# Product quantized convolution on one core: half products of four outputs in a row, and layer 2's preparation moved into layer 1's tail

## The chip, the cores and the metric

The kernel runs on one core of a Trainium2 chip. The metric is the device time of one execution in microseconds. Before the change it is 3702.62 us, the median of three runs (3702.26 to 3704.74).

## The reference

The input x has shape (32, 1024, 14, 14), in fp32. Two residual blocks follow each other. The first, and the only one that the change touches, is a bottleneck of three product quantized ("amm") convolutions, each followed by a batch norm over images and pixels:

```python
def _amm(patches, centroids, lut, inv_temp):
    v = patches.reshape(B, ncb, sub, H * W).transpose(0, 3, 1, 2)
    scores = 2.0 * jnp.einsum('blcs,cks->blck', v, centroids) - jnp.sum(centroids * centroids, -1)[None, None]
    attn = jax.nn.softmax(scores * inv_temp, axis=-1)
    out = jnp.einsum('blck,cko->blo', attn, lut)
    return out.transpose(0, 2, 1).reshape(B, -1, H, W)

out = _amm(x, c1_centroids, c1_lut, c1_invt)             # 1024 -> 256, 256 codebooks of 4 values
out = jax.nn.relu(_bn(out, bn1_g, bn1_b))
out = _amm(_extract3x3(out, 1), c2_centroids, c2_lut, c2_invt)   # 3x3, 256 codebooks of 9 values
out = jax.nn.relu(_bn(out, bn2_g, bn2_b))
out = _amm(out, c3_centroids, c3_lut, c3_invt)           # 256 -> 1024, 64 codebooks of 4 values
out = _bn(out, bn3_g, bn3_b)
return jax.nn.relu(out + identity)

x = x + _L0_conv_ref(_gn(x), ...)    # the block above
x = x + _L1_conv_ref(_gn(x), ...)    # linear attention with rotary positions, and a depthwise 3x3
```

Each codebook has K = 16 centroids: the scores go through a softmax over 16, and its weights multiply rows of a table (`lut`).

## The kernel before, in words

**Stages.** Layers 1, 2 and 3 of the first block run one after the other, each with a batch norm in between, and then the attention block. The order of the instructions on every engine in the three layers is the order in which the program emits them (`manual_schedule`); each engine and each DMA queue works through its own list in order and waits where an operand is missing. The attention block is ordered by a planner (`Plan`), which the change does not touch.

**Layers 1 and 2.** Their work is cut into 128 units: 16 pairs of images (392 pixels) times 8 groups of codebooks. `units` (line 701) interleaves the steps. For a unit, TensorE makes four score tiles of 128 (codebook, centroid) rows in PSUM; ScalarE takes the exponential with a bias (`exponentials`, line 563); DVE transposes so that the 16 centroids lie next to each other (`token_major`), sums over them, takes the reciprocal and transposes it back; GpSimd multiplies (`softmax`, line 585). The softmax weights of a codebook sum to one, so one of the 16 table rows is subtracted from the others (`less`, a matmul with the fixed matrix `less_last` and a copy on ScalarE), and the freed rows hold weights of other codebooks: `spare_rows` (line 691) moves these with small DMAs on the SP queue, and `others` and `keep` in `packed_lut` do the same for the table. Then `lut` adds up table times weights in two PSUM banks. Scores run 4 units (layer 1) or 3 units (layer 2) ahead of the table products, so that the table product of unit u waits only for work that began several units before. `side(i)` and `side2(i)` are called once per unit and place all other work: loads, norms, next tables.

**From layer 1 to layer 2.** After the last unit of layer 1 its norm is finished (`bn_final`). `store_pair` (line 907) applies norm and relu on ScalarE into a padded picture and stores it to DRAM three times, shifted, by SP; `load_patches` (line 933) reads from there what the 3x3 windows need, twelve DMAs for each half of the channels of a pair. Two pieces cannot be taken from these patches alone: the score of layer 2 is a sum of four matmuls of 64 rows on the patches (eight taps, matrix `w8`) and four of 32 rows on the padded picture (the ninth tap, matrix `wm`). The biases (`score_biases`), `w8` (`score_matrices`) and `wm` are made on DVE, between the first patches and the first score. Tables 0 to 3 of layer 2 are reduced (`less`) there too, tables 4 to 7 in `side2`. ScalarE issues a part of the first patches' DMAs, SP all others.

**Layer 3.** The 6272 pixels are cut into 14 chunks of 448. The two groups of codebooks (b = 0, 1) of chunk k + 1 are scored (`score3`, line 1087; four matmuls of 32 rows side by side) while chunk k is multiplied. The freed rows leave seven full tiles of 128 weight rows and one of 64. `spread3` fills the freed rows by small DMAs; `double3` copies the 64 rows of the first tile into its other 64, in two DMAs. A chunk has eight outputs of 128 channels. An output is the sum of seven whole products (`whole`) and a half product of 64 rows. The outputs are taken two at a time (m0 = 0, 2, 4, 6): one half product uses the upper 64 rows and the other the lower 64, so that TensorE does both at once:

```python
for m0 in range(0, CT, 2):
    ...
        whole(m0)
    for m in (m0, m0 + 1):
        r = slice(64 * (m - m0), 64 * (m - m0) + 64)
        product(m, 0, r, ...)
        whole(m0 + 1)
```

After a pair, ScalarE copies the outputs out of PSUM and DVE gathers statistics. The first scores (b = 0) of the next chunk stand before the chunk's first output, the second (b = 1) after output 0; their softmax follows outputs 1 and 3. PSUM has four banks for scores, three for products and one (`ps_tr`) for small things.

Of the kernel before, what the change touches and what calls it, by code (L numbers as in the profile page):

```python
# [10 lines left out]
F32 = mybir.dt.float32  # L11
AF = mybir.ActivationFunctionType
ALU = mybir.AluOpType
# [4 lines left out]
P = 128  # L18
C = 1024
CT = C // P  # L20
# [130 lines left out]
def conv_preact_kernel(ctx: ExitStack, tc: tile.TileContext, a: dict, out: bass.AP):  # L151
# [177 lines left out]
    SHIFT = 32.0  # L329

    def centre(pool, i, name, v, k):

        rows, groups = v.shape[:2]
        mean = pool.tile([rows, groups], F32, tag=f"cmean{i}{name}", name=f"cmean{i}{name}")
        t = pool.tile([rows, 1], F32, tag=f"cinvt{i}{name}", name=f"cinvt{i}{name}")
        nc.vector.tensor_scalar(t, invs[i][:rows], k, None, ALU.mult)
        nc.vector.tensor_reduce(mean, v, AX.X, ALU.add)
        nc.vector.tensor_scalar(mean, mean, t, 1.0 / KC, ALU.mult, ALU.mult)
        nc.vector.scalar_tensor_tensor(v, v, t, bc(mean, 2, KC), ALU.mult, ALU.subtract)

    def score_matrices(pool, i, name, raw, mask):


        rows, groups = raw.shape[:2]
        w = pool.tile([rows, groups, P], F32, tag=f"cw{i}{name}", name=f"cw{i}{name}")
        centre(pool, i, name, raw, 2.0)
        for g in range(0, groups, 4):
            m = min(4, groups - g)
            nc.vector.tensor_tensor(
                w[:, g : g + m].rearrange("p g (c k) -> p g c k", k=KC),  # L350
                raw[:, g : g + m].unsqueeze(2).to_broadcast([rows, m, 8, KC]),
                mask.unsqueeze(1).unsqueeze(3).to_broadcast([rows, m, 8, KC]),
                ALU.mult,
            )
        return w

    def score_biases(ps_tr, pool, tmp, i, raw, rows, groups, mask, per, order=None):

# [12 lines left out]
        cols = sq  # L371
        bias = pool.tile([P, n], F32, tag=f"cbias{i}", name=f"cbias{i}")
        nc.vector.tensor_copy(spread.rearrange("p (c k) -> p c k", k=KC), bc(mask, 2, KC))
# [12 lines left out]
        def biases():  # L386
# [5 lines left out]
            nc.vector.tensor_tensor(pv, pv, bc(kmask, 1, n), ALU.mult)  # L392
            b = pool.tile([P, n], F32, tag=f"cb{i}", name=f"cb{i}")
            nc.vector.tensor_reduce(b, pv, AX.X, ALU.add)
# [96 lines left out]
    def layers(exact, early=None):  # L491
# [143 lines left out]
        tsp = two.enter_context(tc.tile_pool(name="p12t", bufs=1))  # L635

        def unit_tiles(n):

# [61 lines left out]

        def units(ahead, ts, pool, luts, score, bias, dst, stats, side, last, halve=False):

# [27 lines left out]
            for i in range(-ahead, n):  # L730
# [8 lines left out]
                if 0 <= u < n:  # L739
# [4 lines left out]
                        *tts.pop(u),  # L744
                        spare=spares[u // 4 % 2] if u % 4 == 0 else None,
                    )
                    spare_rows(ts, u)
# [12 lines left out]
        with ExitStack() as s:  # L760
            once = s.enter_context(tc.tile_pool(name="p1c", bufs=1))
            xp = s.enter_context(tc.tile_pool(name="p1x", bufs=3))
            sm = s.enter_context(tc.tile_pool(name="p1s", bufs=2))
# [11 lines left out]
            def load(p):  # L775
                def piece():
                    xts[p] = load_x(xp, p)
                    v = slice(2 * p, 2 * p + 2)
# [59 lines left out]
            for b in range(2):  # L838
                luts[b][1]()
            xts[1] = load_x(xp, 1)  # L840
            for b in range(2, 8):
# [31 lines left out]
            def score1(u):  # L873
                p, b = divmod(u, 8)
                scs = []
                for j in range(4):
# [3 lines left out]
                    scs.append(sc)  # L880
                return scs

            units(
# [15 lines left out]
        with ExitStack() as s:  # L899
# [51 lines left out]
            luts2[7][1]()  # L951
            load_patches(0, 0, 1, engines=(nc.sync, nc.scalar))
            store_pair(0, 1)
            luts2[2][2]()
            load_patches(0, 1, 3)
            luts2[3][2]()
            for b in range(4):
                luts2[b][4]()
            bias2, biases = score_biases(
                ps_tr,  # L960
                once,
                st,
                2,
                raw[2],
                72,
                32,
                mask2,
                1,
                lambda t, src=False: t.rearrange("p (h j b) -> p h b j", h=2, j=4)
                if src  # L970
                else t.rearrange("p (h b j) -> p h b j", h=2, b=4),
            )
            w8 = score_matrices(once, 2, "8", raw8, mask64)
            biases()
            warm(5, pads[0][:, :N2])

            centre(once, 2, "1", raw1, 2.0)
            wm = once.tile([P, 2, 4, P], F32, tag="wm", name="wm")
            for h in range(2):
                nc.vector.tensor_tensor(  # L980
                    wm[:, h].rearrange("p b (c k) -> p b c k", k=KC),
                    raw1[:, h].unsqueeze(1).unsqueeze(2).to_broadcast([P, 4, 8, KC]),
                    mask32.rearrange("p (b c) -> p b c", c=8)
                    .unsqueeze(3)
                    .to_broadcast([P, 4, 8, KC]),
                    ALU.mult,
                )

# [30 lines left out]
            def side2(i):  # L1019

                for b in range(4, 8):
                    if i == max(b - 7, -ahead):
                        luts2[b][2]()
                    if i == max(b - 4, 0):
                        luts2[b][4]()
                if i == max(-2, -ahead):
                    luts2[4][3]()
                if i == -ahead:
# [12 lines left out]
            def next_lut3(b):  # L1041
# [15 lines left out]
                side2,  # L1057
                lambda h: bn_final(once, stats2, 2, [h], sc2, bi2),
            )
            next_lut3(7)  # L1060
# [5 lines left out]
        with ExitStack() as s:  # L1066
# [78 lines left out]
            relu3(1, 1)  # L1145
            nxt = [score3(1, 0)]
            rows = sum(map(split3, t3), [])
# [6 lines left out]
            spread3(rows, range(4, 8))  # L1154
            double3(rows[0])
            for k in range(NCH):
                more = k + 1 < NCH
                if more and k:
                    nxt = [score3(k + 1, 0)]
                elif not more and not exact:  # L1160
                    add_up(2, 2 * NCH)
                    again = overflow(once)
# [5 lines left out]
                def product(m, g, r=slice(0, P), start=False, stop=False):  # L1168
# [6 lines left out]
                    )  # L1175

                def whole(m):
                    for g in range(1, CT):
                        product(m, g, start=m % 2 == 0 and g == 1, stop=m % 2 == 1 and g == 7)

                for m0 in range(0, CT, 2):
                    for m in range(m0, m0 + 2 + (k + m0 == 0)):
                        if m not in pos:
                            pos[m] = ps_po.tile([P, 512], F32, tag="po", name="po3")[:, :NC]

                    if k + m0 == 0:
                        for g in range(1, CT):
                            for m in range(3):
                                product(m, g, start=g == 1)
                    elif k > 0 or m0 != 2:  # L1190
                        whole(m0)
                    for m in (m0, m0 + 1):
                        r = slice(64 * (m - m0), 64 * (m - m0) + 64)
                        product(
                            m, 0, r, start=m > m0 and k + m0 > 0, stop=m == m0 or k + m0 == 0
                        )
                    if k + m0 > 0:
                        whole(m0 + 1)
                    for m in (m0, m0 + 1):
                        nc.scalar.copy(o[:, m, :], pos[m])  # L1200
                        nc.vector.bn_stats(stats3[:, m, k, :], o[:, m, :])  # L1201
                        if not more:
                            bn_sum(mv3[:, m, :], stats3, m)
                        if more and m == 0:
                            nxt.append(score3(k + 1, 1))
                        if m in (4, 5):
                            relu3(k + 2, m - 4)
                        if more and m in (1, 3):
                            t = nxt[m // 2]
                            softmax(st, 2 * k + 2 + m // 2, t, *token_major(st, t))  # L1210
                            if m == 1:
                                then = split3(t)
                                spread3(then, (1, 2, 3))
                            else:
                                then += split3(t)
                                spread3(then, range(4, 8))
                                double3(then[0])
                nc.sync.dma_start(o3d[:, :, k * NC : (k + 1) * NC], o)
                if more:
                    rows = then  # L1220
            bn_final(once, None, 3, range(CT), sc3, bi3, mv3)
# [804 lines left out]
```

## Time and profile before

| what | us |
|---|---|
| median of three runs | 3702.62 |
| the profiled execution, own time | 3700.99 |
| its span | 3699.2 |
| TensorE busy | 3626.1 |
| DVE busy | 2979.5 |
| GpSimd busy | 2307.5 |
| ScalarE busy | 1717.9 |
| layer 1's last table product ends, TensorE's next work begins | 836.7 |
| first score of layer 2 | 856.3 |
| first scores of layer 3 | 1845.1 |
| first product of layer 3 | 1860.3 |
| last chunk's products begin | 2501.4 |

In the lines of the profile, PE is TensorE, PEld its loading of weights, DVE VectorE, ACT ScalarE, POOL GpSimd, and SPq and ACTq the DMA queues that SyncE and ScalarE issue. In a timeline line the first number is the start in us from the span's beginning and the second its length; then come engine, line of the kernel, instruction, what it writes and reads with shapes, and the number of instructions that were merged into the line. In brackets stands how long the engine idled before and what released it. In a group line the numbers after the bar are busy us in all and the mean ns of one instruction, then the idle time before them. An fp32 matmul is recorded as two instructions, one for each of its two passes, each with a load of weights.

### The profile page before, as it was taken

The page shows a single profiled execution, that of the slowest core. Times are in us where ns is not written, and L with a number is a line of the kernel's source. Part 1 is how long each engine was busy: PE and PEld are TensorE (multiplying, and loading weights), DVE is VectorE, ACT ScalarE, POOL GpSimd, SP SyncE. Part 2 cuts the span into 40 slices and gives each one's busy share as a digit, 9 for nine tenths or more (in the row PEclk, how much of TensorE's full clock was granted, in tenths as well). Part 3 has the DMA queues.
Part 4 walks back from the last instruction along what each step waited for, and adds up shares of the span by engine and source line. Part 5 has one row for each costly group of instructions (what it writes and reads, how often), then busy time and mean ns, then how long its engine had stood idle before and what let it go on. Part 6 is the DMA issues. An engine that isn't in the chain of part 4 may idle for free. (4 is left out here: it accounts for less than half of the span.)

```text
span 3699.2 us, 49702 instructions
## 1 busy us (share of the span) xinstructions
PE 3626.1 (98%) x16229; PEld 1999.0 (54%) x16229; DVE 2979.5 (81%) x4291; ACT 1717.9 (46%) x3895; POOL 2307.5 (62%) x1398
## 2 busy tenths in 40 slices
PE   8999999999999999999999999998999999999999
PEld 4555555554554445445444444444666666666666
DVE  8999999987888888888753334333799999999996
ACT  5555555543333333333322222213776676676675
POOL 6999999993454445445421111111988888888887
PEclk9999999999999999999999999999999999999999
DMA  3111111115444434444221111103123233233321
GB/s 110 43 46 44 43 37 32 43 33 134 89 92 87 94 75 94 85 95 84 72 51 53 45 45 45 38 33 130 44 79 93 82 87 91 86 84 85 90 75 44
DMA packets 238331, 260.14 MB, mean 70 GB/s; under 512 B 33380, under 2 KB 235692, under 8 KB 238064
## 3 DMA queue, kind: packets, MB, share of 16 engines
q1 hardware_dynamic: 237280, 256.51, 26.2%
q8 instruction: 131, 2.15, 0.3%
q14 instruction: 136, 1.11, 0.1%
q10 hardware_dynamic: 784, 0.37, 0.0%
HBM read 164.04 MB, written 77.09 MB: 65 GB/s over the span
## 5 line engine op out<-in xcount | busy, mean ns | idle before, releaser
L612 POOL TENSOR_TENSOR t<-t,r 128x1664 f32<-128x1664 f32 (+3 forms) x288 | 1008.5, 3502 | 952.0 <-DVE r L605 771.7
L717 PE MATMUL po<-t,lut 128*128 128x392 f32 x3840 | 1332.1, 499 | 2.7 <-DMA t<-spare 2.5
L717 PEld LDWEIGHTS po<-t,lut 128*128 128x128 f32 x3840 | 710.5, 190 | 593.3 <-issue 122.0
L566 ACT ACTIVATE t<-sc,cbias 128x392 f32<-128x392 f32 (+1 forms) x1136 | 580.0, 594 | 946.2 <-issue 476.1
L1536 PE MATMUL mm<-y,lut 128*128 128x392 f32 x2048 | 710.4, 493 | 0.1
L1169 PE MATMUL po<-t,lut 128*128 128x448 f32 (+1 forms) x1792 | 662.1, 551 | 1.6 <-issue 1.6
L578 DVE STREAM_TRANSPOSE tt<-t 128x1664 f32<-128x1664 f32 (+1 forms) x284 | 541.8, 1908 | 105.4 <-ACT t L566 99.7
L605 DVE STREAM_TRANSPOSE r<-rc 128x1664 f32<-128x1664 f32 (+1 forms) x284 | 546.5, 1924 | 20.8 <-DVE rc L599 0.5
L1758 DVE SCALAR_TENSOR_TENSOR pa<-y,lepe_w,pa 128x406 f32<-128x406 f32 x900 | 537.4, 637 | 3.8 <-PE pa L1740 0.3
L1536 PEld LDWEIGHTS mm<-y,lut 128*128 128x128 f32 x2048 | 370.4, 188 | 243.1 <-issue 6.1
L1169 PEld LDWEIGHTS po<-t,lut 128*128 128x128 f32 (+1 forms) x1792 | 308.7, 189 | 352.0 <-issue 351.3
L597 DVE TENSOR_REDUCE sm<-tt 128x104 f32<-128x832 f32 (+2 forms) x284 | 423.2, 1490 | 7.6 <-POOL tt L581 2.0
L1201 DVE BATCH_NORM_STATS2 stats<-o 128x6 f32<-128x448 f32 x112 | 68.9, 617 | 432.0 <-ACT o L1200 432.0
L581 POOL TENSOR_TENSOR tt<-tt 128x832 f32<-128x832 f32 x128 | 248.4, 1941 | 9.3 <-DVE tt L578 9.3
L599 DVE RECIPROCAL rc<-sm 128x104 f32<-128x104 f32 (+1 forms) x284 | 229.4, 808 | 9.8
L1200 ACT COPY o<-po 128x448 f32<-128x448 f32 x112 | 59.2, 530 | 326.4 <-PE po L1169 278.5
L999 PE MATMUL sc<-patch,cw 64*128 64x392 f32 x1024 | 204.0, 514 | 1.4 <-ACT lut L675 1.4
L614 ACT ACTIVATE sm<-sm 128x104 f32<-128x104 f32 (+1 forms) x284 | 84.9, 299 | 215.3 <-DVE rc L599 213.6
L999 PEld LDWEIGHTS sc<-patch,cw 64*128 64x128 f32 x1024 | 87.5, 184 | 109.5 <-issue 62.0
L1721 POOL TENSOR_TENSOR qr<-qr,zb 128x784 f32<-128x784 f32 x64 | 117.8, 1852 | 42.7 <-DMA zb<-zd 35.1
L1389 ACT ACTIVATE w<-x,tb,gn_a 128x196 f32<-128x196 f32 x248 | 128.3, 517 | 33.4 <-DVE x L1403 19.9
L1545 ACT ACTIVATE e<-mm,kbd 128x392 f32<-128x392 f32 x128 | 74.6, 583 | 145.2 <-PE mm L1536 143.7
(191 smaller groups left out, 4103.7 us busy)
## 6 DMA issues: line engine op xcount, KB each, us to landing
patch<-h1d SPq DMA_DIRECT2D x248, 162.8 KB
x<-in_x_dram SPq DMA_DIRECT2D x32, 784.0 KB
o3d<-o SPq DMA_DIRECT2D x14, 1792.0 KB
x<-in_x_dram SPq DMA_DIRECT2D x64, 392.0 KB
out_dram<-x SPq DMA_DIRECT2D x64, 392.0 KB
o<-o3d SPq DMA_DIRECT2D x62, 392.0 KB
h1d<-pad SPq DMA_DIRECT2D x96, 225.0 KB
t<-spare SPq DMA_DIRECT2D x960, 12.2 KB
```

The lines of the kernel that those rows point to most:

```text
L566: nc.scalar.activation(t[:, j, : sc.shape[1]], sc, AF.Identity if exact else AF.Exp, bias=bias[:, j : j + 1],)
L578: nc.vector.transpose(tt, tf)
L581: nc.gpsimd.tensor_tensor(tv[:, :, :8], tv[:, :, :8], tv[:, :, 8:], ALU.add)
L597: nc.vector.tensor_reduce(sm, tv, AX.X, ALU.add)
L599: nc.vector.reciprocal(rc, sm)
L605: nc.vector.transpose(r, bc(rc, 2, KC))
L612: nc.gpsimd.tensor_tensor(tf[:, v], tf[:, v], r[:, v], ALU.mult)
L717: nc.tensor.matmul(po[h], luts[b][:, j, h * P : (h + 1) * P], ts[u % len(ts)][:, j, :N2], start=(b == 0 and j == j0), stop=(b == 7 and j = ...
L999: nc.tensor.matmul(sc, w8[r, 8 * h + 4 * (j // 2) + g], grid(pbuf[n % NPB][r, j // 2, g]), start=True, stop=False,)
L1169: nc.tensor.matmul(pos[m], luts[g][r, m * P : (m + 1) * P], rows[g][r], start=start, stop=stop,)
L1536: nc.tensor.matmul(pv(), w[kt][:, m0 : m0 + P], ywin(p, first + kt), start=(kt == 0), stop=(kt == 3),)
L1758: nc.vector.scalar_tensor_tensor(acc, neighbours(p, c, offset(k)), lw[:, c, k : k + 1], acc, ALU.mult, ALU.add,)
```

## The change

It has four parts.

1. **Layer 3: halves of four outputs together.** The outputs are taken four at a time (m0 = 0, 4). The order on TensorE is: the whole products of m0, the scores of the next chunk (b = 0 with m0 = 0, b = 1 with m0 = 4), the half products of m0 to m0 + 3, then the whole products of the other three. The softmax of the scores follows the copy and statistics of output m0. The fourth output in work uses the bank of `ps_tr`. In chunk 0 the first four outputs have their whole products first and their halves last.
2. **Layer 2's matrices in layer 1's tail.** `matrices2` makes `w8`, `wm` and the biases at step 125 of layer 1's 128 steps (the bias matmul at step 127), in a tile that a third of layer 1's x tiles used before; `Cut` hands out pieces of a tile. Layer 1's x ring of three becomes a ring of two and a pool of one that lasts through layer 2.
3. **First patches by two queues.** The remaining three quarters of the first patches are issued by SP and ScalarE too, before the second `store_pair`. Tables 2 to 7 are reduced one step or more later in `side2`; `warm` has eight matmuls instead of five.
4. **First weights in pieces.** The GpSimd multiplication of layer 2's units 0 and 1 is split into three pieces each.

```diff
-            xp = s.enter_context(tc.tile_pool(name="p1x", bufs=3))
+            xp = s.enter_context(tc.tile_pool(name="p1x", bufs=2))
...
-                    xts[p] = load_x(xp, p)
+                    xts[p] = load_x(kept if p % 3 == 1 else xp, p)
...
+            def matrices2():
+                room = kept.tile([P, CT, N2], F32, tag="x", name="room2")
...
+                cut = Cut(st.tile([P, 4 * NCP], F32, tag="tt", name="cut2", bufs=n))
+                bias2, biases = score_biases(
...
+                parts[2] = score_matrices(cut, 2, "8", raw8, mask64, w8), wm, bias2
+                centre(cut, 2, "1", raw1, 2.0)
+                for h in range(2):
+                    nc.vector.tensor_tensor(
+                        wm[:, h].rearrange("p b (c k) -> p b c k", k=KC),
...
+                at(8 * NP - 1, biases)
+
+            at(8 * NP - 3, matrices2)
...
-            load_patches(0, 0, 1, engines=(nc.sync, nc.scalar))
+            both = nc.sync, nc.scalar
+            load_patches(0, 0, 1, engines=both)
+            load_patches(0, 1, 3, engines=both)
             store_pair(0, 1)
-            luts2[2][2]()
-            load_patches(0, 1, 3)
-            luts2[3][2]()
-            for b in range(4):
-                luts2[b][4]()
-            bias2, biases = score_biases(
...
-            w8 = score_matrices(once, 2, "8", raw8, mask64)
-            biases()
-            warm(5, pads[0][:, :N2])
...
+            luts2[0][4]()
+            luts2[1][4]()
+            warm(8, pads[0][:, :N2])
+            w8, wm, bias2 = parts[2]
...
-                for b in range(4, 8):
-                    if i == max(b - 7, -ahead):
+                for b in range(2, 8):
+                    if i == max(b - 6 if b > 2 else -3, -ahead):
                         luts2[b][2]()
-                    if i == max(b - 4, 0):
+                    if i == max(b - 3 if b > 3 else b - 4, -ahead):
                         luts2[b][4]()
-                if i == max(-2, -ahead):
-                    luts2[4][3]()
+                    if b == 4 and i == -1:
+                        luts2[4][3]()
...
+                steps={0: (1, 1, 1), 1: (1, 1, 2)},
...
-            nxt = [score3(1, 0)]
+            nxt = score3(1, 0)
...
                 def whole(m):
                     for g in range(1, CT):
-                        product(m, g, start=m % 2 == 0 and g == 1, stop=m % 2 == 1 and g == 7)
+                        product(m, g, start=m % 4 == 0 and g == 1, stop=m % 4 > 0 and g == 7)
+
+                def halves(m0):
+                    for m in (m0, m0 + 1):
                         if m not in pos:
+                            pool, tag = (ps_tr, "tr") if m % 4 == 3 else (ps_po, "po")
+                            pos[m] = pool.tile([P, 512], F32, tag=tag, name="po3")[:, :NC]
+                        r = slice(64 * (m - m0), 64 * (m - m0) + 64)
+                        first = k + m0 // 4 == 0
+                        product(m, 0, r, start=m % 4 > 0 and not first, stop=m % 4 == 0 or first)
...
+                for m0 in (0, 4):
...
+                        whole(m0)
+                    t = None
+                    if more and (k or m0):
+                        t = score3(k + 1, m0 // 4)
+                    elif more:
+                        t = nxt
+                    halves(m0)
+                    halves(m0 + 2)
+                    out(m0)
+                    if t is not None:
+                        then(m0 // 4, t)
+                    for m in range(m0 + 1, m0 + 4):
+                        if k + m0 > 0:
+                            whole(m)
+                        out(m)
```

## The prediction

> **What bounds the kernel now.** I read the page's shares first, then TensorE's groups with shapes kept apart, then the timeline in the two places that the change touches. The page:
>
> ```profile
> span 3699.2 us, 49702 instructions
> ...
> PE 3626.1 (98%) x16229; PEld 1999.0 (54%) x16229; DVE 2979.5 (81%) x4291; ACT 1717.9 (46%) x3895; POOL 2307.5 (62%) x1398
> ```
>
> TensorE is busy for 98% of the span, and only 73 us are idle anywhere. So a saving needs less TensorE time in a stage, or less idle time at a joint. TensorE's groups in layer 3, by form:
>
> ```profile
> L1169 PE MATMUL po<-t,lut 128*128 128x448 f32 x1568 | 612.5, 545 | 1.6 <-issue 1.6
> L1169 PE MATMUL po<-t,lut 64*128 64x448 f32 x224 | 57.3, 588 | 0.0
> L1093 PE MATMUL sc<-out,cw 32*128 32x448 f32 x224 | 29.0, 586 | 1.3 <-ACT out L1083 1.3
> ```
>
> Every product counts twice here (14 chunks x 8 outputs x 7 rows = 784, shown as 1568): fp32 runs in two passes. Layer 3 practically never waits; only its TensorE work can shrink. What a block of short matmuls costs is seen in the weight loads, whose starts give the beat (timeline, weight loads of layer 3):
>
> ```profile
> 2062.21 0.19 PEld L1169 LDWEIGHTS po<-t,lut 128*128 128x128 f32 x1 [0.19 <-issue]
> 2063.05 0.30 PEld L1169 LDWEIGHTS po<-t,lut 64*128 64x128 f32 x4 [0.65 <-issue]
> 2064.01 0.30 PEld L1169 LDWEIGHTS po<-t,lut 128*128 128x128 f32 x2 [0.65 <-issue]
> 2064.49 0.19 PEld L1169 LDWEIGHTS po<-t,lut 128*128 128x128 f32 x1 [0.19 <-issue]
> ```
>
> Full passes follow each other every 0.375 us. Around a pair of half products the starts are 0.84, 0.96 and 0.48 us apart: 2.28 us instead of 3 x 0.375 = 1.125. So a block of one half pair adds 1.16 us, of which two passes (0.75) are work and 0.41 is the change into half rows and back. A block of scores (32 rows, four side by side) has the same gaps, 0.85 and 0.96, at 2069.47. A chunk holds four half blocks and two score blocks: 112 x 0.375 + 6 x 1.16 = 49.0 us, and chunk periods by the timeline are 49.02 us (2057.59 to 2106.61). The model holds.
>
> Does a second half pair right behind the first pay the change again? Layer 2 shows it:
>
> ```profile
> 1502.51 0.96 PEld L999 LDWEIGHTS sc<-patch,cw 64*128 64x128 f32 x8 [0.56 <-issue]
> 1504.03 0.31 PEld L1008 LDWEIGHTS sc<-pad,wm 32*128 32x128 f32 x8 [0.56 <-issue]
> 1504.90 1.28 PEld L717 LDWEIGHTS po<-t,lut 128*128 128x128 f32 x5 [0.56 <-issue]
> ```
>
> Eight 64-row loads lie within 0.96 us, of which the last group takes 0.30: the second pair starts 0.66 us after the first, two passes at layer 2's 0.328. So nothing is paid between pairs. From the second pair to the 32-row block it is 1504.03 - 1503.17 = 0.86 us, 0.20 more than two passes: changing between 64 and 32 rows costs 0.20.
>
> The other place is the start of layer 2 (timeline, several engines):
>
> ```profile
> 842.54 4.48 ACTq L940 DMA_DIRECT2D patch<-h1d  x6
> 847.07 0.71 ACT L909 ACTIVATE pad<-out,bi,sc 128x392 f32<-128x392 f32 x1 [6.17 <-DMA patch<-h1d]
> 856.34 0.96 PEld L999 LDWEIGHTS sc<-patch,cw 64*128 64x128 f32 x8 [0.56 <-DVE wm L980]
> 858.81 2.02 ACT L566 ACTIVATE t<-sc,cbias 128x392 f32<-128x392 f32 x4 [7.81 <-PE sc L1008]
> 880.08 4.74 PE L717 MATMUL po<-t,lut 128*128 128x392 f32 x12
> 887.14 2.93 PEld L717 LDWEIGHTS po<-t,lut 128*128 128x128 f32 x10 [0.56 <-issue]
> ```
>
> The first score waits for DVE's wm, the last matrix of layer 2. Its patches are there long before: by windows of half a microsecond the DMA burst that carries them ends at 848.5. From 880 on (first table product) TensorE runs without gaps, unit after unit of 7.85 us; 887.14 is unit 1's first product, my mark for the joint.
>
> **What the Trainium skill says.** "TensorEngine Tiling (Array Packing)", Key Properties: changing the tiling mode, not just the tile, drains TensorE. The trace agrees: 0.41 us out and back, nothing between two 64-row pairs. "TensorE: Matmul & The Clock Gate", Part 3, says that tiles of different row groups run side by side; four 64-row loads within 0.30 us agree. "DMA: Bandwidth & Descriptors", Issuing engines are not separate DMA queues: a second issuing engine saves only issue time. Here twelve loads take 6.16 us on SP alone (849.67) and six on each of SP and ACT 4.48 us, while the DMA engines are busy 0.8 to 0.9 at 180 to 190 GB/s (852 to 858): I count little for the second queue.
>
> **The change part by part.**
>
> *Layer 3.* Per half chunk, three blocks (score, two half pairs) become one. Before: 3 x 1.16 = 3.49 us. After: six passes 2.25, into short rows and back 0.41, score to halves 0.20: 2.86. That is 0.63 per half chunk, 1.26 per chunk, 15.1 over the 12 chunks with both scores. Chunk 0 goes from five blocks (5 x 0.41) to one of halves and one with scores (0.41 + 0.61): 1.0 less. The last has no scores: four blocks to two, 0.8 less. One new wait: in chunk 0 the copies of outputs 1 to 3 sit on ACT behind the sum of the softmax, and halves 4 to 7 need their banks; I take 0.5 once. Sum: -16.4. The trace shows 64 to 32 rows, not 32 to 64: free it would be -21, at a full 0.41 -11.
>
> What moves later is the second score of the next chunk, from after output 0 to after the first products of output 4. Its chain, from the score's first load as 0: exps end 3.3 (as after the score at 2056.63: first exp 1.10 later, 2.21 long in all), copy 3.8, statistics 4.5, transpose, sum, reciprocal, transpose 11.6 (2083.52 to 2090.64 is 7.1), GpSimd 15.7 (3.97 at 2090.78), then SP: four row spreads 0.6 apart, the two doublings 2.5 and 4.15 after GpSimd's end:
>
> ```profile
> 2090.78 3.97 POOL L612 TENSOR_TENSOR t<-t,r 128x1792 f32<-128x1792 f32 x1 [5.75 <-DVE r L605]
> ...
> 2097.26 0.51 SPq L1116 DMA_DIRECT2D t<-t  x1
> 2098.90 0.51 SPq L1117 DMA_DIRECT2D t<-t  x1
> ```
>
> L1117 needs L1116 landed, so such a small DMA lands within 1.7. The first spread row is there at 17.4, the doubled rows at 21.6. The next chunk begins at 2.66 + 42 x 0.375 - 0.27 = 18.1; its seventh pass (row group 4, the first of these) is at 20.4, its halves at 24.8. Both have about 3 us to spare. So the new order costs nothing; without that cover every microsecond is paid 13 times. The first half's chain has a whole half chunk more.
>
> *Layer 1's tail.* DVE is idle from 823.5 to 834.8 (11.28 us before L754). The moved work took 6.30 (840.11 to 846.41) + 1.65 (biases) + 2.12 (centre, wm) = 10.1 us: it ends near 833.6, just inside. If it overran, the norm and everything after would move by as much. The bias matmul (two passes of 512, 0.43 each at full clock) comes before TensorE's last unit, where nothing hides it: +0.9. Moving the x tiles to two pools leaves a ring of three: nothing.
>
> *Start of layer 2.* The first score no longer waits for DVE: it runs at 848.7. But ACT now issues twelve DMAs instead of six (0.75 each: 842.5 to 851.5), and only then pad 1's relu, so the exps start at about 852.3, not 858.81: -6.5. Behind them ACT has four copies of tables 2 and 3 (0.55 each), which were done earlier before; TensorE's second piece of table 3 waits for the first of them, and score 1 comes at 856. Then exps 1 at 858.5 (863.12 before), copies of table 4 and two relus, exps 2 at 863.5 (868.09), exps 3 at 868.1 (875.87). Rows of unit 0: DVE 854.4 to 861.0, GpSimd in pieces of 1.0 until 865.2, SP's three spreads until 865.8, landed 868. Table 6's two pieces then the first products at 871 instead of 880.1. SP before that: three stores at 852.3, two tables, six patch loads 856.6 to 859.6 (their store lands 2.5 later, as 840.02 to 842.52), three more, the spreads, six stores, three loads until 871.7, unit 1's spreads until 874.3. Table 7's four passes and their wait for a bank now stand before unit 1: its first product at 880.4 instead of 887.14, -6.7. Splitting the multiplication moves two units' rows earlier by 1 to 3 us at 0.1 us of GpSimd; TensorE is not waiting for them then. With the +0.9: -5.8. Ends: -9 if SP and ACT keep up better, +1 if the twelve issues hold ACT until the DMA engines have drained (1302 KB at 190 GB/s, 6.9 us) and the stores behind delay all that follows.
>
> Sum: -16.4 - 5.8 = -22.2 against the profiled execution's own 3701.0 (span 3699.2), so 3678.8; that execution lies 1.6 below the median of the runs, so a median of 3680.4.
>
> **Rivals.** (1) The start gives nothing: SP is in order, and pad 1's stores, the loads behind them and unit 0's spreads end as late as before, because ACT's relu now follows twelve issues. For: SP and DMA are dense from 850 to 869. Against: the stretch 870 to 874 has no DMA traffic at all. Only layer 3 stays: 3686. (2) Blocks do not merge: 32 to 64 rows, or every pair of outputs, drains as from full rows. For: no view has score before halves. Against: layer 2's two pairs. Then -5.8 alone: 3697. (3) Slower: in layer 3 the second score's rows come after their use. One output later (DVE takes the transpose only after output 5's copy, 5.25 us) turns 3.0 spare into 2.3 late, x 13 = +30: 3710. It outweighs the gain from 4.7 us of delay on. Against: each step of the chain is measured.
>
> **How the numbers follow.** Forecast 0.68, (1) 0.18, (2) 0.06, (3) 0.08. A difference below 0.2% (7.4 us) could not be told from none in a measurement of this kernel; so faster 0.86 (forecast and (1)), same 0.06 (2), slower 0.08 (3). The range 3671 to 3692: below it both unknowns at their good ends (-21 and -9), above it lie (2), (3) and a dear row change together with a gainless start (-11); all of that is about 0.2.
>
> **What would show it.** Chunk period 47.8 instead of 49.0; two short-row blocks per chunk, with 2.25 us of passes each; no TensorE wait on layer 3's t rows. DVE's moved rows between 823 and 834, the norm unmoved but for 0.9. First score near 849, exps 0 near 852, unit 1's product 44 us after layer 1's last instead of 50. I am wrong if TensorE waits for a DMA at a chunk's seventh pass, or if ACT's issues last beyond 854.

## The result, and the profile after

The changed kernel takes 3695.44 us (median of 16 runs, 3690.64 to 3699.21), the kernel before 3700.80 (16 runs, 3697.59 to 3704.74). The ratio is 0.9984, with a 95% interval of 0.9977 to 0.9991: 5.4 us faster, where 22 were forecast. The profiled execution of the changed kernel took 3693.2 us. Its page, shares of busy time:

```profile
span 3691.1 us, 49689 instructions
...
PE 3609.0 (98%) x16235; PEld 2003.4 (54%) x16235; DVE 2984.0 (81%) x4291; ACT 1725.3 (47%) x3895; POOL 2307.5 (63%) x1402
```

TensorE works 17.1 us less than before, but the span is only 8.1 us shorter: 9 us of new idle time ate half of the saving. The groups of layer 3 by form:

```profile
L1198 PE MATMUL po<-t,lut 128*128 128x448 f32 x1568 | 599.2, 542 | 1.2 <-DMA t<-t 1.2
L1198 PE MATMUL po<-t,lut 64*128 64x448 f32 x224 | 49.8, 562 | 0.0
L1123 PE MATMUL sc<-out,cw 32*128 32x448 f32 x224 | 29.0, 586 | 1.3 <-ACT out L1113 1.3
```

The same instructions take 20.8 us less (612.5 + 57.3 before); where one group overlaps the next the time is counted in both, so this is more than the stage saves (14.6 us, in the table below). In the weight loads of a half chunk one sees how (timeline, weight loads of layer 3; scores, then two pairs of halves, then whole products):

```profile
2080.31 0.19 PEld L1198 LDWEIGHTS po<-t,lut 128*128 128x128 f32 x1 [0.19 <-issue]
2081.15 0.31 PEld L1123 LDWEIGHTS sc<-out,cw 32*128 32x128 f32 x8 [0.65 <-issue]
2082.11 0.30 PEld L1198 LDWEIGHTS po<-t,lut 64*128 64x128 f32 x4 [0.65 <-issue]
2082.59 0.19 PEld L1198 LDWEIGHTS po<-t,lut 64*128 64x128 f32 x2 [0.18 <-issue]
2082.97 0.19 PEld L1198 LDWEIGHTS po<-t,lut 64*128 64x128 f32 x2 [0.18 <-issue]
2083.82 0.30 PEld L1198 LDWEIGHTS po<-t,lut 128*128 128x128 f32 x2 [0.65 <-issue]
2084.30 0.19 PEld L1198 LDWEIGHTS po<-t,lut 128*128 128x128 f32 x1 [0.19 <-issue]
```

From the last whole load to the third of the next ones it is 3.99 us, of which 1.125 would pass without the block: the block adds 2.87 us. From scores to halves it is 0.96, 0.21 above two passes. Half chunks follow each other every 23.91 us, a chunk takes 47.82.

The start of layer 2 (timeline):

```profile
841.60 9.26 ACTq L997 DMA_DIRECT2D patch<-h1d  x12
845.90 1.02 PE L1028 MATMUL sc<-patch,room 64*128 64x392 f32 x4 [1.58 <-DMA patch<-h1d]
851.81 2.00 ACT L579 ACTIVATE t<-sc,room 128x392 f32<-128x392 f32 x4
870.52 4.11 PE L732 MATMUL po<-t,lut 128*128 128x392 f32 x12
877.36 0.89 PE L1028 MATMUL sc<-patch,room 64*128 64x392 f32 x2 [1.22 <-DMA patch<-h1d]
879.79 3.78 PE L689 MATMUL sc<-lut,less_last 128*128 128x512 f32 x4 [0.66 <-ACT t L579]
883.36 6.73 PE L732 MATMUL po<-t,lut 128*128 128x392 f32 x16
```

The first score is 10.4 us earlier, the first table product 9.6, but unit 1's first product (883.36) only 3.8, and unit 5's score 2.6 (890.02 against 892.61), of which 1.2 is layer 1's earlier end.

The execution cut into stages, in us (first column: start of the last matmul of layer 1's table products; layer 3: from its first score to the first matmul on tb, which opens the attention block; last: from there to the end):

| kernel | layer 1's last product starts | from there to unit 5's score in layer 2 | to layer 3's first score | layer 3 | attention |
|---|---|---|---|---|---|
| before | 836.4 | 56.3 | 952.5 | 714.5 | 1139.6 |
| after | 835.1 | 54.9 | 953.2 | 699.9 | 1148.0 |

So layers 1 to 3 together gained 16.5 us, and the attention block, of which the change touches no line, lost 8.4. Its waits on TensorE, before:

```profile
PE mm L1421 <- DVE tb L1257: 9.5, 1, 9.5
PE mm L1598 <- ACT kt L1601: 8.4, 27, 1.0
```

and after, where line 1644 is line 1598 of before:

```profile
PE mm L1644 <- DVE kv L1690: 8.2, 6, 1.4
PE mm L1644 <- ACT kt L1647: 7.4, 11, 0.8
```

Six new waits for DVE's `kv`, 8.2 us in all, about what is lost. In both traces the instructions of the attention block are the same in number, but their order is not: ScalarE's two sequences agree for 115 instructions and then part. The order is the planner's, and the planner holds a clue:

```python
        engines = {p[0] for p in self.pieces}
...
            for e in engines:
```

The first line makes a set of names ("PE", "DVE" and so on), and the loop asks the engines in the set's order at every step. That order follows from Python's hashing of strings, which differs from one process to the next. A piece that is marked `port` may not start while another engine holds the port, so it matters who is asked first where both DVE and GpSimd have such a piece. Of the orders of the five engines that were built, those with DVE before GpSimd give programs of one size and those with GpSimd before DVE programs of another. The profiled kernel before carries the sequence of GpSimd first, all 1654 instructions of ScalarE alike; the profiled kernel after that of DVE first. The profiles of the experiments below bear this out on every engine: in the block TensorE, DVE, ScalarE and GpSimd each have one sequence in the eleven profiles with GpSimd first, where the block takes 1138.3 to 1141.1 us, and one in the three with DVE first, where it takes 1147.3 to 1148.0.

### The profile page after: what moved, and what is told of

Read it like the earlier page. It is cut to its first block, busy times and chain, and to the rows that moved or that the text cites. A ratio compares the mean times of both kernels' runs of the same rounds, so it can differ in the third digit from the quotient of the medians.

```text
span 3691.1 us, 49689 instructions
## 1 busy us (share of the span) xinstructions
PE 3609.0 (98%) x16235; PEld 2003.4 (54%) x16235; DVE 2984.0 (81%) x4291; ACT 1725.3 (47%) x3895; POOL 2307.5 (63%) x1402
## 5 line engine op out<-in xcount | busy, mean ns | idle before, releaser
L625 POOL TENSOR_TENSOR t<-t,r 128x1664 f32<-128x1664 f32 (+5 forms) x292 | 1009.0, 3457 | 952.6 <-DVE r L618 751.9
L1198 PE MATMUL po<-t,lut 128*128 128x448 f32 (+1 forms) x1792 | 646.8, 545 | 1.2 <-DMA t<-t 1.2
L1804 DVE SCALAR_TENSOR_TENSOR pa<-y,lepe_w,pa 128x406 f32<-128x406 f32 x900 | 540.5, 636 | 19.4 <-PE pa L1786 17.1
L579 ACT ACTIVATE t<-sc,room 128x392 f32<-128x392 f32 x512 | 258.6, 588 | 593.1 <-issue 374.1
L579 ACT ACTIVATE t<-sc,cbias 128x392 f32<-128x392 f32 (+1 forms) x624 | 320.5, 597 | 405.6 <-PE sc L895 144.3
L1028 PE MATMUL sc<-patch,room 64*128 64x392 f32 x1024 | 206.1, 517 | 3.1 <-DMA patch<-h1d 3.1
L1028 PEld LDWEIGHTS sc<-patch,room 64*128 64x128 f32 x1024 | 88.4, 185 | 112.1 <-issue 66.9
L1548 ACT ACTIVATE y<-x,gb,ga 128x196 f32<-128x196 f32 x256 | 122.5, 541 | 46.2 <-POOL gb L1511 46.2
## 6 DMA issues: line engine op xcount, KB each, us to landing
patch<-h1d SPq DMA_DIRECT2D x248, 162.8 KB
```

The costliest lines, as they stand in the source:

```text
L579: nc.scalar.activation(t[:, j, : sc.shape[1]], sc, AF.Identity if exact else AF.Exp, bias=bias[:, j : j + 1],)
L625: nc.gpsimd.tensor_tensor(tf[:, v], tf[:, v], r[:, v], ALU.mult)
L1028: nc.tensor.matmul(sc, w8[r, 8 * h + 4 * (j // 2) + g], grid(pbuf[n % NPB][r, j // 2, g]), start=True, stop=False,)
L1198: nc.tensor.matmul(pos[m], luts[g][r, m * P : (m + 1) * P], rows[g][r], start=start, stop=stop,)
L1804: nc.vector.scalar_tensor_tensor(acc, neighbours(p, c, offset(k)), lw[:, c, k : k + 1], acc, ALU.mult, ALU.add,)
```

## The experiments

In every kernel from here on the set is replaced by a list, in one of two orders. This is the list for "GpSimd first"; the one for "DVE first" is `['PE', 'DVE', 'ACT', 'POOL', 'SP']`:

```diff
-        engines = {p[0] for p in self.pieces}
+        engines = ['PE', 'POOL', 'ACT', 'DVE', 'SP']
```

**Is it the order or the change?** Kernel before, GpSimd first:

> The kernel before, with the planner's loop over the engines in a fixed order that asks GpSimd before DVE; this gives the attention block the order that the profiled kernel before had. Theory A (the planner's order in the attention block depends on the build, and costs what layers 1 to 3 gained): equal to the kernel before where that was built in this order, about 3700.8 us, attention from the first matmul on tb to the end 1139 to 1141 us. Theory B (the change itself slows the attention block): the order of the planner makes no difference, so all that matters is before or after: also 3700.8.

Measured: 3701.59 us (11 runs, 3696.33 to 3702.43).

Kernel before, DVE first:

> The kernel before, with the planner asking DVE before GpSimd; this gives the attention block the order that the profiled kernel after had. Theory A: 8 to 11 us slower than with GpSimd first, about 3710 us, attention about 1148 us. Theory B: no difference, 3701 us, attention 1140 us.

Measured: 3709.86 us (13 runs, 3707.77 to 3714.71). Attention 1147.3 us against 1139.3. The waits of TensorE in this kernel, whose source is that of before, show the line again that the changed kernel had shown:

```profile
PE mm L1598 <- DVE kv L1644: 8.2, 6, 1.4
...
PE mm L1598 <- ACT kt L1601: 7.3, 11, 0.8
```

The busy time of the block by windows, GpSimd first and then DVE first, says that the instructions are the same in number and TensorE is busy for the same time, so that what it loses is idle time:

```profile
2560.90:3700.10 1139.20, 1121.56 (x7022) 757.25 (x7022) 1049.88 (x2510) 786.46 (x1654) 941.14 (x862) 1.00 0.29 84
```

```profile
2564.00:3711.30 1147.30, 1120.69 (x7022) 755.87 (x7022) 1049.39 (x2510) 796.44 (x1654) 940.21 (x862) 1.00 0.28 83
```

(Columns: stretch, its length, then busy us and instructions of TensorE, its weight loads, DVE, ScalarE and GpSimd; clock, DMA share, GB/s.) TensorE idles 17.6 us in the first and 26.6 in the second. (ScalarE is busy 10 us longer in the second; why, no run shows.)

Changed kernel, GpSimd first:

> The changed kernel, with the planner asking GpSimd before DVE. Theory A: layers 1 to 3 keep their gain of 16.5 us and attention takes 1140 us: 3684 us, a ratio of 0.9955 to the kernel before in the same order. Theory B: attention stays at 1148 us, 3695 us.

Measured: 3686.35 us (5 runs, 3683.12 to 3688.65), attention 1138.3.

Changed kernel, DVE first:

> The changed kernel, with the planner asking DVE before GpSimd, as the profiled one had it. Both theories: about 3695 us, attention about 1148 us. Theory A puts it 16 us below the kernel before in the same order, theory B 5 us below either order of the kernel before.

Measured: 3697.47 us (5 runs, 3692.86 to 3698.42), attention 1147.5.

Theory A stands on all four, to within 2.5 us, and theory B falls. In the same order the change is worth 15.2 us (3701.59 to 3686.35) or 12.4 (3709.86 to 3697.47), ratios of 0.996 and 0.997, with ranges of runs that do not meet; the order is worth 8.3 and 11.1. The kernel before that was timed alongside these and the later kernels came out at 3710.28, 3710.36 and 3708.44, the value of DVE first (by the time alone; it was not profiled), although its source is the one that gave 3700.8 in the comparison above. So the comparison above set a kernel before with GpSimd first against a kernel after with DVE first. All that follows has GpSimd first and is compared with 3701.59 and 3686.35. The kernels came in three batches on three chips, and that kernel before gave the three values just named, so a difference between batches carries an uncertainty of about 2 us.

**Which part gains?** The new order of layer 3 alone (the three last pieces of the diff):

> The kernel before with only the new order of layer 3 (half products of four outputs together), planner asking GpSimd first. By the traces, layer 3 from its first scores to the first matmul on tb took 714.5 us before and 699.9 to 702.8 after. Theory A (layer 3 carries nearly the whole gain): 3687 to 3690 us, 12 to 14.5 below the kernel before in the same order (3701.6). Theory B (the layers share the gain as forecast): 3685, and the other half alone 3696.

Measured: 3684.93 us (5 runs, 3682.62 to 3689.09), 16.7 below the kernel before; layer 3 in 700.0 us. This is at theory B's number and 2 us under theory A's. The trace puts 14.5 us of it in layer 3, as theory A has it; of the rest, 1.9 lie in the start of layer 2 (54.8 us up to unit 5's score against 56.7), which this edit does not touch. One stretch at half the full clock of TensorE, 6.8 us long, that the kernel before has there (from 875.9) is missing in this profile.

Everything but the new order of layer 3:

> The changed kernel with the old order of layer 3: only layer 2's matrices in layer 1's tail, the patches by two queues and the weights in pieces, planner asking GpSimd first. Theory A: 1 to 3 us below the kernel before in the same order (3699 to 3700.5), layer 2's sixth score about 54.5 us after layer 1's last product instead of 56.7. Theory B: 5.8 below, 3696.

Measured: 3700.14 us (6 runs, 3695.78 to 3702.61), 1.5 below, unit 5's score 55.4 us after layer 1. Here theory A's number holds and theory B's 3696 does not. Together: the gain is layer 3's. The start of layer 2 gives nothing that the times can tell: 1.5 us less with the old layer 3, but 1.4 us more with the new one (3684.93 without it, 3686.35 with it). In the traces the stretch up to unit 5's score takes 54.8 to 57.0 us in five kernels with the old start (mean 56.0), and 54.2 to 55.9 in five with the new one (mean 55.0).

**Why does the start give so little?** The new start lies on forecast until its first table product, and loses then. Unit 4's score stops in its midst for 1.22 us for the last patches of the half pair. In the SP queue's timeline (changed kernel as profiled) these three loads stand behind the six stores of the next pair:

```profile
866.68 3.81 SPq L977 DMA_DIRECT2D h1d<-pad  x6
870.54 1.49 SPq L997 DMA_DIRECT2D patch<-h1d  x3
```

and the DMA engines are full of those stores while the loads wait, and then carry the loads themselves (windows of 2 us, columns as above):

```profile
868.00:870.00 2.00, 1.34 (x7) 0.68 (x4) 1.97 (x3) 1.94 (x4) 1.73 (x2) 1.00 0.99 303
870.00:872.00 2.00, 2.00 (x7) 1.11 (x6) 1.97 (x2) 0.08 (x1) 2.00 (x2) 1.00 0.98 314
872.00:874.00 2.00, 2.00 (x7) 1.17 (x7) 1.90 (x2) 1.22 (x4) 0.27 (x1) 1.00 0.89 190
874.00:876.00 2.00, 2.00 (x8) 0.67 (x7) 2.00 (x2) 0.12 (x1) 1.16 (x1) 1.00 0.69 118
876.00:878.00 2.00, 0.78 (x3) 0.29 (x2) 1.97 (x2) 0.00 (x0) 2.00 (x1) 1.00 0.32 86
```

Issued by 872.0, they are used at 877.4. Then TensorE's granted clock falls to half of the full one from 879.1 to 885.9: table 7's four passes take 3.78 us (1.98 at full clock) and unit 1's products 6.73 (5.53). That is 1.2 + 1.8 + 1.2 = 4.2 us. Such a stretch is not new here: the kernel before has one of the same length, from 874.5 to 881.3, and table 7 takes as long in it (timeline, before):

```profile
876.51 3.78 PE L674 MATMUL sc<-lut,less_last 128*128 128x512 f32 x4 [0.64 <-ACT t L566]
```

The experiment takes away what makes the score wait:

```diff
-                    load_patches(n + 1, js=((0, 1), (2,), (3,))[g])
+                    load_patches(n + 1, js=(((0, 1), (2,), (3,)) if n else ((0, 1), (2, 3), ()))[g])
```

> The changed kernel, planner asking GpSimd first, and the last three patch loads of layer 2's second half pair issued one unit earlier, ahead of the first units' spreads and of the six stores of the next pair. Theory C (unit 4's score waits 1.2 us for these patches, and the stretch at half clock that follows comes from the gaps around it): the wait is gone and, with the half clock gone or shorter, 2 to 4.5 us less than the changed kernel in the same order (3682 to 3684). Theory D (only the wait itself counts, the half clock comes anyway): 1 us less, 3685.

Measured: 3680.24 us (5 runs, 3678.83 to 3681.85), 6.1 below the changed kernel. Its TensorE:

```profile
874.94 4.19 PE L732 MATMUL po<-t,lut 128*128 128x392 f32 x12 [1.62 <-DMA t<-spare]
879.06 1.59 PE L1028 MATMUL sc<-patch,room 64*128 64x392 f32 x8
880.58 0.94 PE L1037 MATMUL sc<-pad,room 32*128 32x392 f32 x8
882.18 1.98 PE L689 MATMUL sc<-lut,less_last 128*128 128x512 f32 x4 [0.66 <-ACT t L579]
884.00 5.43 PE L732 MATMUL po<-t,lut 128*128 128x392 f32 x16
```

Unit 4's score no longer waits, there is no half clock behind it, and unit 5's score comes 50.6 us after layer 1 instead of 54.2: 3.6 us, in theory C's range. The other profiles agree: in all five with the start as written (1.1 to 3.0 us of waiting in unit 4's score) a half-clock stretch of 3.4 to 10.2 us begins in the wait or soon after it, and in none of the four with these loads moved ahead is there a wait or such a stretch at this place. Moving the loads has a price too: unit 0's rows come later, and the first table product waits 1.62 us for them. Of the 6.1, about 3 lie in layer 3 (699.9 us against 702.8), which the edit doesn't touch; there, up to the end of its products, this profile had one stretch of half clock of 3.4 us where the other had 3.4 and 6.8. "TensorE: Matmul & The Clock Gate", Part 1 of the Trainium skill, has the array at half rate after an idle window of about 3.4 us; the stretches in these stages are indeed 3.4, 6.8 or 10.2 us long, but they came behind gaps of 1.1 to 3.0 us too, shorter than that window, and not every time: none followed the 1.62 us above. What decides it stays open.

**Layer 3's own gaps.** In chunk 3 a transpose for the attention tables (`ph`) stands at the beginning, waiting for nine small DVE operations. Before and after:

```profile
2008.51 0.33 PE L477 MATMUL ph<-ident,hp 128*128 128x128 f32 x1 [1.48 <-DVE hp L475]
```

```profile
2003.86 0.30 PE L490 MATMUL ph<-ident,hp 128*128 128x128 f32 x1 [2.54 <-DVE hp L488]
```

The scores that used to stand ahead of it (1.0 us) have moved, so TensorE waits 1.06 longer. In the last chunk the overflow check makes it idle for 1.85 us and, while its result is read, for 1.17 us (timeline, after):

```profile
2484.32 0.19 PE L635 MATMUL pf<-ones,good 128*1 128x1 f32 x2 [1.85 <-DVE good L633]
2485.68 47.83 PE L1198 MATMUL po<-t,lut 128*128 128x448 f32 x128 [1.17 <-DMA t<-t]
```

The trace names a DMA for the second. These gaps are not the change's doing (1.76 and 1.60 us before). Both jobs were moved to where their inputs are long ready; `count_bad`, a new function, is the second part of `overflow`, the matmul and its result as an integer, without reading it:

```diff
...
-                    again = overflow(once)
-                if early and k > 0:
+                    good = overflow(once)
+                if early and k in (1, 2):
                     early.pop(0)(ps_tr)
...
                     else:
                         whole(m0)
+                    if not (more or exact or m0):
+                        bad = count_bad(once, good)
+                    if early and k == 3 and m0 == 4:
+                        early.pop(0)(ps_tr)
...
                     halves(m0 + 2)
+                    if not (more or exact or m0):
+                        again = nc.values_load(bad[0:1, 0:1], min_val=0, max_val=P)
                     out(m0)
```

> The changed kernel, planner asking GpSimd first, and two small jobs of layer 3 moved off the chunk's beginning: the transpose for the attention tables comes in chunk 3 behind the products of output 4, and of the overflow check in the last chunk the one-column matmul comes behind the first seven products and the reading of its result behind the half products. TensorE was idle 2.5 us at the first and 3.1 us at the second, and ran at half clock for 3.4 to 6.8 us after the second and in some profiles after the first. Theory C (idle time and half clock both go): 6 to 10 us less than the changed kernel in the same order (3676 to 3680). Theory D (the waits only move): less than 2 us.

Measured: 3678.74 us (5 runs, 3676.99 to 3679.93), 7.6 below. Layer 3 takes 692.1 us, with no half clock from its first score to its last product, and none of the three gaps is left, the one that the trace had put down to a DMA among them. Theory C holds: 2.5 + 3.0 us of idle time, and for the rest the half clock that is gone. Little of this idle time had come with the change: the kernel before has 1.48 + 3.36 us of it, and 3.4 us at half clock behind it.

**Both amendments:**

> The changed kernel, planner asking GpSimd first, with both amendments: layer 2's last three patch loads one unit earlier, and layer 3's two small jobs moved off the chunk's beginning. By stages in the traces the amendments are worth 3.6 us (unit 5's score 50.6 instead of 54.2 us after layer 1's last product) and 7.8 to 10.7 us (layer 3 in 692.1 us instead of 699.9 to 702.8). If they add up: 3672 to 3675 us. If the half clock only moves elsewhere: 3677 to 3679.

Measured: 3673.22 us (5 runs, 3671.90 to 3681.14), 13.1 below the changed kernel and 28.4 below the kernel before in the same order (both from another batch); by the stages the gains add up (50.8 us to unit 5's score, layer 3 in 692.1). Against the kernel before that was timed alongside, at the value of DVE first, the ratio is 0.9910 (0.9896 to 0.9923).

**What the parts of the start are worth, amended.** The second queue taken back, and with it the earlier place ahead of the second picture:

```diff
-            load_patches(0, 1, 3, engines=both)
             store_pair(0, 1)
+            load_patches(0, 1, 3)
```

> The kernel with both amendments, but the last three quarters of layer 2's first patches are issued by SP alone and after the second picture's relu, as before the change. ScalarE is then free 4.5 us earlier for that relu and the first exponentials, but these patches come 3 to 4 us later. Theory E (ScalarE's issuing holds up the start): 2 to 4 us faster than with two queues. Theory F (the patches of units 1 to 3 set the start): 1 to 4 us slower. Neither (SP's later loads and stores set it): within 1 us.

Measured: 3676.60 us (5 runs, 3675.23 to 3680.90). The 3.4 us more are unclear by the times alone (0.9904 to 0.9931 against 0.9896 to 0.9923); in the trace unit 5's score comes at 53.5 instead of 50.8, and the scores wait four times for patches, 4.0 us in all, instead of twice, 3.4. This speaks for theory F. Whether the second queue counts or the earlier place of the loads, this run cannot tell, since it takes both back.

The weights in pieces taken back (`steps` left out):

> The kernel with both amendments, but the weights of layer 2's first two units multiplied as before the change, not in pieces. Forecast: the first table product waits for nothing of it, so within 1 us. If the pieces are needed (in the profile with earlier patches the first table product waited 1.6 us for unit 0's spread rows): 1 to 3 us slower.

Measured: 3673.70 us (4 runs, 3672.45 to 3675.70), unit 5's score at 50.3: the pieces are worth nothing, as forecast.

The whole start taken back, layer 3 as amended:

> Only the new order of layer 3, with its two small jobs moved, and layers 1 and 2 as before; planner asking GpSimd first. Layer 3 in 692 us. Against the kernel with both amendments this leaves out the whole work on layer 2's start: if that start is worth its amended 5 us, 3677 to 3679 us; if it is worth nothing, equal.

Measured: 3679.25 us (5 runs, 3676.03 to 3680.72), 6.0 above the version with the amended start. So the start is worth about 6 us once the patches come in time, and as it was written nothing that the times can tell (about 1 us by the stage).

## Why the prediction was wrong

The two profiles differ by 8.1 us where 22.2 were forecast. Of the 14 us between, 8.4 are lost in the attention block, 5.3 in the start of layer 2 and 0.7 in the rest of it, 1.8 in layer 3; layer 1's end, 2.1 us earlier than forecast, gives some back. The two failures are therefore the start of layer 2 and what follows layer 3.

**Layer 3, -16.4: right in its mechanism, and near in size.** The stage gained 14.5 to 14.6 us in two of the profiles. Alone the new order measured -16.7, but some 2 us of that lie outside layer 3, so the closer agreement is luck. By its terms: 3.99 us from load to load give a block of 2.87 (forecast 2.86), 0.21 for 32 to 64 rows (0.20, the unknown), a chunk of 47.82 (47.8). The chain of the second scores lies where it was put (timeline of the changed kernel, the score's first load at 2033.32):

```profile
2044.91 3.97 POOL L625 TENSOR_TENSOR t<-t,r 128x1792 f32<-128x1792 f32 x1 [19.97 <-DVE r L618]
...
2053.15 0.52 SPq L1147 DMA_DIRECT2D t<-t  x1
```

GpSimd ends 15.6 after it (15.7 forecast), the last doubling is issued at 19.8 (19.9), and TensorE doesn't wait: rival 3 falls. Rival 2 falls with the chunk period. Missed was one consequence of the moved scores: they had covered the table transpose of chunk 3 (1.06 us, and 1.7 more where 3.4 us at half clock followed, in two profiles; with a longer stretch behind the overflow check as well, layer 3 takes 702.8 and 702.9 us there).

**Layer 1's tail, +0.9: right.** The bias matmul takes 0.86 us (829.33 to 830.19) ahead of the last unit. DVE's moved work ends at 833.7 (833.6 forecast), just as the norm begins, and hides as said. In layer 1's end itself 0.9 us cannot be seen (see the last section).

**Start of layer 2, -6.7: the step that failed is "three loads until 871.7".** The forecast took it that loads issued by 871.7 (872.0 measured) are there for unit 4's score. It had counted the six stores ahead of them only for SP's time to issue, 3.8 us, and not for the DMA engines, which these 1350 KB filled until about 872; and it had put the loads' own transfer (three of 162.8 KB, carried from about 872 to 876) at nothing. How much of the wait is due to each, no run separates. Nearly all before this step is within 1 us of the forecast: the exponentials at 851.8 (852.3), the first table product at 870.5 (871); only the first score was earlier than said, 845.9 (848.7). Unit 1's first product then came 47.9 us after layer 1's end, where 44 was forecast. The clock was not in the sum either: it had table 7's passes at full clock, and these and unit 1's products lost 3.0 us at half clock, 2.5 times the wait. As the kernel before had lost about as much there, the -6.7 had counted, without saying so, on this stretch to go. With these loads moved ahead, wait and stretch are gone and the stage gains 5.6 to 6.1 us (56.3 to 56.8 down to 50.6): the sum was right for a start whose patches come in time. What was measured instead is rival 1, the start giving next to nothing, but not for its reason, ScalarE's relu behind twelve issues: the relu came at 851.2, as forecast, and the first table product 9.6 us earlier than before. The argument against that rival, no DMA traffic from 870 to 874 (0 and 13 GB/s before), held for the old queue only: the changed kernel moves 314 and 190 GB/s there. Neither of the two signs of being wrong that were named came (ScalarE's issues end at 850.9). The remark that the second queue counts little remains untested by itself; queue and earlier place together were worth 2.6 us in the trace.

**What follows layer 3, not costed: wrong by 8.4 us.** The sum took the 1139.6 us from the end of layer 3 on as fixed, because no edit lies there. It is fixed for one order of the planner only, and the two programs compared had different ones. With the order held, the change gives -15.2 us, that is 3687.4 from the median of before, inside the range that was given, but at rival 1's 3686 rather than the forecast's 3680: it is layer 3's gain alone. Nothing in the trace of before could show the other order; the loop over a set in the code could have.

## What to carry to other kernels

In this kernel TensorE paid for each change between full-height and short matmuls (0.41 us in and out), not for each short one; where a kernel has such runs, put scores and half products into one and count the runs. When a transfer is moved in a queue, ask what the DMA engines will be carrying then, and how long the transfer itself takes, not only when the queue gets to it. And before a difference of half a per cent is put down to an edit, make sure that a program which orders its own instructions comes out the same in both builds: a set of strings is enough to move 8 us.

## What the runs showed of the hardware that was not expected

- A run of short rows costs 0.41 us in and out for full height, 0.20 to 0.21 between 64 and 32 rows in either direction, and nothing between pairs of 64.
- A gap of 1.2 us on TensorE was followed by 6.8 us at half clock, and cost 4.2 us in all; in five profiles gaps of 1.1 to 3.0 us at this place came with 3.4 to 10.2 us at half clock, and in four with the gap closed there was none. Behind the gap of 2.5 us in chunk 3 the half clock came in two profiles and not in three others.
- Layer 1's last product lies anywhere from 836.4 to 839.1 us in the profiles of kernels whose layer 1 is the one of before, so a single execution of the whole cannot carry a difference of 3 us. Stages of the trace vary less, but they vary too: the old start of layer 2 took 54.8 to 57.0 us.
